# Image statistics on GpSimd, waiting rounds on ScalarE, and four circuit operations a step, in a diagonal LSTM with a quantum layer

## The chip, the cores and the metric

The kernel runs on one core of a Trainium2 chip. The metric is device time in microseconds, the median of the runs. Engines are named as in the profile: PE is TensorE's matrix products, PEld its weight loads, DVE is VectorE, ACT is ScalarE, POOL is GpSimd, SP is the engine that issues most of the DMAs. "L202" is line 202 of the kernel.

## The reference

The input x has the shape (16 images, 128 channels, 64 rows, 64 columns), all in float32. Two layers follow each other, each with a group norm in front and a residual around it.

```python
x = x + lstm(_gn(x), w_is, b_is, w_ss, b_ss)
x = x + quantum(_gn(x), pre_w, pre_b, q_weights, post_w, post_b)

def _gn(v, G=32, eps=1e-5):          # mean and variance over 4 channels and all pixels of an image
    ...
    return ((g - m) / jnp.sqrt(s + eps)).reshape(v.shape)

# layer 0: row i is shifted right by i columns (127 in all), then a scan over the columns
def step(carry, ist):
    h, c = carry
    h_shift = jnp.pad(h, ((0, 0), (0, 0), (1, 0)))[:, :, :-1]     # h of the row above
    s_s = einsum(w_ss[:, :, 0], h_shift) + einsum(w_ss[:, :, 1], h) + b_ss
    gates = ist + s_s                                             # ist = w_is @ column + b_is
    o, f, ig = sigmoid(gates[:, :3 * C]) in three parts
    g = jnp.tanh(gates[:, 3 * C:])
    c_new = f * c + ig * g
    h_new = o * jnp.tanh(c_new)

# layer 1: at each pixel four angles pre_w @ x + pre_b enter a circuit of four qubits with two
# layers of rotations (q_weights) and CNOTs; four expectation values go through post_w, post_b
```

Two facts matter here. First, row i sees i columns of zeros before its image begins. In these its state doesn't depend on the image: it is the same for all images and for all rows that still wait, and it follows from the biases and from the sum of the two taps of `w_ss`. Second, the rotations and the first CNOTs depend on `q_weights` alone, so a small matrix of amplitudes can be prepared once, at any time before layer 1 begins.

## The kernel before

**Preparation** (L220 to L430) loads the images into `ring`, a buffer of 40 rows an image; the 24 rows behind go through seven small buffers (three `rest` tiles and four `spare` tiles). On each 512-element piece VectorE runs `bn_stats` (L287), eight for an image; then `aggregated` (L290), one `bn_aggr` an image, turns the eight results into the mean and variance of a channel in `mv1`. SP's loads of the small buffers wait for the statistics that free them.

In the same stretch runs the chain of **waiting rounds**, `inv_step` (L191 to L212): round j takes the waiting rows' state j to state j+1. A state is one column of 128 channels in `hinv` and `cinv`. A round is eight products on TensorE (L199; two for each of four gates, since a float32 product takes two passes), four gate activations on ScalarE (L202, in the order f, i, g, o, the bias being a column operand), three one-column operations on POOL (L205 f·c, L206 i·g, L207 their sum), tanh of c (L209) and h = o·tanh(c) (L210, an Identity whose scale is the column of o). Behind each round's products stand two holding products, `keep` (L182), that keep TensorE busy; one reads a piece of the image in the ring, the other the weights `wsT`. 33 rounds (`EARLY`) are made here, spread over the images by a loop; later states are made inside the scan.

The order on every engine is the order in which the code issues (a manual schedule). So in the first round POOL first runs `coefficients` (L313 to L319) and the clearing of the state buffers (L366, L367), and only then the round's L205. ScalarE copies the transposed weights wxT, w0T and w1T (L326) behind the first round's h; TensorE transposes them into two alternating PSUM tiles, so that the third waits for the copy of the first.

At the **hand-over** POOL copies states 0 and 33 into the scan's h (L402, L403), TensorE makes the first step's products with them (L408), then three holding products (L182), then the group mean (L147), VectorE and ScalarE make 1/sqrt of the variance, and POOL normalises the first columns (L576, L588).

**The scan** has 160 steps in the skewed order. In a step TensorE makes the gate products (L783, L597), ScalarE copies and activates (L833, L802, L862), VectorE adds and multiplies (L798, L850, L858, L861, L868), POOL adds the residual (L641) and normalises the columns two steps ahead (L576 to L588). From step 33 on VectorE also takes three operations a step of the circuit (L441, L452, L470, L483), a generator of 120 operations: 8 rotations of 11, 4 CNOTs of 6, 8 products at the end. They stand behind the step's differences (L625) and in front of L798, which is the first of the chain that the step waits for. When four rows are finished, their statistics for the second norm (L732, 16 of them) are issued in the same place, up to six a step.

**Layer 1** then runs over all pixels, and stores.

Of the kernel before, what the change touches and what calls it, by code (L numbers as in the profile page):

```python
# [11 lines left out]
F32 = mybir.dt.float32  # L12
AF = mybir.ActivationFunctionType
# [3 lines left out]
P = 128  # L17
NB = 16
NH = 64
NW = 64  # L20
SLOTS = 32
# [4 lines left out]
BLOCK = ROWS * NW  # L26
CHUNK = 2 * BLOCK
EARLY = 33
FIRST = 8
STRIP = 4  # L30
FEW = 96
# [10 lines left out]
GO, GF, GI, GG = 0, 1, 2, 3  # L42
FUNC = {GO: AF.Sigmoid, GF: AF.Sigmoid, GI: AF.Sigmoid, GG: AF.Tanh}
# [38 lines left out]
def kernel(  # L82
# [16 lines left out]
    nc = tc.nc  # L99
# [10 lines left out]
    ring = const.tile([P, NB, RING * NW], F32, name="ring")  # L110
# [18 lines left out]
    w_image = const.tile([P, NB, 48], F32, name="w_image")  # L129
    b_image = const.tile([P, NB], F32, name="b_image")  # L130
    b_theta = const.tile([P, 1], F32, name="b_theta")
    w_amp = const.tile([P, 2, 128], F32, name="w_amp")
# [27 lines left out]
    small = ctx.enter_context(tc.tile_pool(name="small", bufs=2))  # L160
    with ExitStack() as scan:
# [4 lines left out]
        wsT = wpool.tile([P, 512], F32, name="wsT")  # L166
# [12 lines left out]
        def keep(pool, tag, v):  # L179

            ps = pool.tile([P, v.shape[-1]], F32, name=nc.get_next_instruction_name(), tag=tag)
            nc.tensor.matmul(ps, lhsT=wsT[:, 0:P], rhs=v, start=True, stop=True)  # L182
# [8 lines left out]
        def inv_step(j, pool):  # L191


            ps = {}
            rhs = hinv[:, j : j + 1].to_broadcast([P, P])
            for g in ORDER:
                ps[g] = pool.tile([P, P], F32, name=f"inv_ps{j}_{g}", tag=f"inv{g}")
                w = wsT[:, g * 128 : (g + 1) * 128]
                nc.tensor.matmul(ps[g], lhsT=w, rhs=rhs, start=True, stop=True)  # L199
            ac = small.tile([P, 4], F32, name=f"inv_a{j}", tag="inv_a")  # L200
            for g in ORDER:
                nc.scalar.activation(ac[:, g : g + 1], ps[g][:, 0:1], FUNC[g], bias=bias[:, g : g + 1])  # L202
            ig = small.tile([P, 2], F32, name=f"inv_i{j}", tag="inv_i")
            c = cinv[:, j + 1 : j + 2]
            nc.gpsimd.tensor_mul(ig[:, 0:1], ac[:, GF : GF + 1], cinv[:, j : j + 1])  # L205
            nc.gpsimd.tensor_mul(ig[:, 1:2], ac[:, GI : GI + 1], ac[:, GG : GG + 1])  # L206
            nc.gpsimd.tensor_add(c, ig[:, 0:1], ig[:, 1:2])  # L207
            th = small.tile([P, 1], F32, name=f"inv_t{j}", tag="inv_t")
            nc.scalar.activation(th, c, AF.Tanh)  # L209
            nc.scalar.activation(  # L210
                hinv[:, j + 1 : j + 2], th, AF.Identity, scale=ac[:, GO : GO + 1]
            )  # L212

        def above(v, a, b):

# [4 lines left out]
        with ExitStack() as prep:  # L220
# [68 lines left out]
            def aggregated(b):  # L289
                nc.vector.bn_aggr(  # L290
                    mv1[:, b, :], stats[:, b, 0:8].rearrange("p g s -> p (g s)")
                )


            q3 = qw.rearrange("p (n a) -> p a n", a=3)
            ang = pp.tile([P, 2, 3, 8], F32, name="ang")
            rnd = pp.tile([P, 2, 3, 8], F32, name="rnd")
# [14 lines left out]
            def coefficients():  # L312
                nc.gpsimd.tensor_mul(co[:, 0], trig[:, 0, 0, :], trig[:, 0, 2, :])  # L313
                nc.gpsimd.tensor_mul(co[:, 1], trig[:, 1, 0, :], trig[:, 0, 2, :])
                nc.gpsimd.tensor_mul(co[:, 2], trig[:, 0, 1, :], trig[:, 1, 2, :])
                nc.gpsimd.tensor_mul(co[:, 3], trig[:, 1, 1, :], trig[:, 1, 2, :])
                nc.gpsimd.tensor_scalar_mul(co[:, 4:8], co[:, 0:4], -1.0)
                nc.gpsimd.tensor_copy(cur[:, 0], expand)
                nc.gpsimd.memset(cur[:, 1], 0.0)  # L319

# [38 lines left out]
            for i in range(2):  # L359
                v = ws_n[i]  # L360
                nc.vector.tensor_add(sum_n[:, 2 * i : 2 * i + 2], v[:, :, 0::2], v[:, :, 1::2])
            transposed("wsT", wsT, lambda g: sum_n[:, g, :])
            biases()
            coefficients()
            for v in (*hst, *xns, none):
                nc.gpsimd.memset(v, 0.0)  # L366
            nc.gpsimd.memset(w_image, 0.0)  # L367

            for k in (3, 4, 0):
                statistics(0, k)  # L370
# [1 line left out]

            between = [angle_weights, output_weights]
            done = 0
            for b in range(NB):
                while b < NB - 1 and done * (NB - 1) < EARLY * (b + 1):
                    inv_step(done, ps_inv)
                    keep(ps_keep, "keep", ring[:, b, CHUNK : CHUNK + P])
                    keep(ps_keep, "keep", wsT[:, 0:P])
                    if done == 0:  # L380

                        transposed("wxT", wxT, lambda g: wx_n[:, g, :])
                        transposed("w0T", w0T, lambda g: ws_n[g // 2][:, g % 2, 0::2])
                        transposed("w1T", w1T, lambda g: ws_n[g // 2][:, g % 2, 1::2])
                    elif done > 4 and between:
                        between.pop(0)()
                    done += 1
                if b + 2 < NB:
                    rows(b + 2)
                if b + 1 < NB:  # L390
                    behind(b + 1)
                    for k in ORDERED:
                        statistics(b + 1, k)
                for k in (5, 6, 7):
                    statistics(b, k)
                aggregated(b)
            prep_ps.close()


# [373 lines left out]
        def step(t, ps):  # L773
# [36 lines left out]
            elif t:  # L810
                differences(t, now, diff)
                for g in summed:
                    half(g, 0, wsT, now[:, 0])
            if t > SLOTS:
                for _ in range(3):
                    next(steps, None)
            if t + 1 < SLOTS:

# [80 lines left out]
        with tc.manual_schedule():  # L899
            normalised(0)  # L900
            normalised(1)
            ps = gate_ps(0)
            for t in range(NSTEP):
                ps = step(t, ps)
            statistics(10.0, NSTEP)
            for later in sums:
                for _ in later:
                    pass
            residual(NSTEP - 1, hst[NSTEP % 2], nc.vector)
            low_rows(nc.sync, 6, spare[6])  # L910

            warm = small.tile([P, 1], F32, name="warm", tag="inv_t")
            nc.scalar.activation(warm, shift, AF.Sqrt)
            ps = ps_small.tile([P, 2, NB], F32, name="gm3", tag="small")

            def add(to, w, v, start=False):
                nc.tensor.matmul(to, lhsT=w, rhs=v, start=start, stop=True, skip_group_check=True)

            add(ps, by_half, moments, True)
            fill(2)  # L920
            for h in range(2):
                add(ps, by_half, added[:, :, :, h])
                add(ps[:, 1], by_one, inner[:, :, h])
            fill(1)

            v = block(NH - ROWS).rearrange("p i (r w) -> p i r w", w=NW)[:, :, :, NW - STRIP :]
            d, sq = (work.tile([P, NB, ROWS, STRIP], F32, name=f"strip{i}", tag=f"both{i}") for i in range(2))
            m = mean2.unsqueeze(2).unsqueeze(3).to_broadcast([P, NB, ROWS, STRIP])
            nc.vector.tensor_sub(d, v, m)
            nc.vector.tensor_mul(sq, d, d)  # L930
            for i, u in enumerate((d, sq)):
                u = u.rearrange("p i r w -> p i (r w)")
                nc.vector.reduce_sum(strip_sums[:, i], u, axis=mybir.AxisListType.X)
            add(ps, by_one, strip_sums)
# [24 lines left out]
            nc.tensor.matmul(ps, lhsT=w_theta, rhs=mr, start=True, stop=True)  # L959
            nc.vector.tensor_sub(b_image, b_theta.to_broadcast([P, NB]), ps)  # L960
# [219 lines left out]
```

## Time and profile before

| | us |
|---|---|
| median of 3 runs (1411.8 to 1412.43) | 1411.82 |
| the profiled execution | 1411.93 |
| its span, first to last instruction | 1409.8 |
| end of the last image's mean and variance (L290) | 94.54 |
| end of the state 33 (last L210 of the preparation) | 95.36 |
| first group mean (L147) | 100.48 |
| first step's normalised columns on TensorE (L597) | 103.98 |
| first circuit operation in the scan (L441) | 290.14 |
| last circuit operation (L483), start | 628.7 |

A line of the timeline gives the start in us from the beginning of the span, the duration in us, the engine, the line of the code, the operation, output and inputs by name, shapes, and how many neighbours are merged in the line; in brackets stand the idle time of the engine just before and what ended it. Since neighbours are merged, "x4" with 0.93 us is the time from the first one's start to the last one's end. In the first part of the page a row gives busy time, share of the span and number of instructions of each engine; in the fourth, shares of the chain of work that ended last.

A step of the scan in its wide middle takes 8.61 us (from one L625 to the next).

### The profile page before, as it was taken

The page shows a single profiled execution, that of the slowest core. Times are in us where ns is not written, and L with a number is a line of the kernel's source. Part 1 is how long each engine was busy: PE and PEld are TensorE (multiplying, and loading weights), DVE is VectorE, ACT ScalarE, POOL GpSimd, SP SyncE. Part 2 cuts the span into 40 slices and gives each one's busy share as a digit, 9 for nine tenths or more (in the row PEclk, how much of TensorE's full clock was granted, in tenths as well). Part 3 has the DMA queues.
Part 4 walks back from the last instruction along what each step waited for, and adds up shares of the span by engine and source line. Part 5 has one row for each costly group of instructions (what it writes and reads, how often), then busy time and mean ns, then how long its engine had stood idle before and what let it go on. Part 6 is the DMA issues. An engine that isn't in the chain of part 4 may idle for free.

```text
span 1409.8 us, 20064 instructions
## 1 busy us (share of the span) xinstructions
PE 1355.0 (96%) x6046; PEld 967.6 (69%) x6046; DVE 975.5 (69%) x2541; ACT 776.0 (55%) x1852; POOL 887.6 (63%) x1599
## 2 busy tenths in 40 slices
PE   6778999999999999999999999999999999999995
PEld 5658977777777766666677767777776787886332
DVE  7973565566665666887777776666665567876996
ACT  4655666555555555555555555555555566654331
POOL 4225777777777766777777776777777677763300
PEclk9999999999999999999999999999999999999998
DMA  9960000000000000133333100000000000014999
GB/s 339 407 234 2 1 1 1 1 0 1 0 1 1 1 1 1 60 120 120 120 120 120 60 1 1 1 1 0 1 1 0 1 0 1 1 31 143 383 400 358
DMA packets 64075, 107.04 MB, mean 76 GB/s; under 512 B 5040, under 2 KB 32720, under 8 KB 63968
## 3 DMA queue, kind: packets, MB, share of 16 engines
q1 hardware_dynamic: 59328, 94.39, 18.5%
q0 software_dynamic: 3408, 10.58, 2.0%
q8 instruction: 48, 0.79, 0.2%
q10 hardware_dynamic: 1232, 0.80, 0.2%
q14 instruction: 59, 0.48, 0.1%
HBM read 59.61 MB, written 46.14 MB: 75 GB/s over the span
## 4 chain that ended last, share of the span: by engine, by line
PE 82%; DVE 4%; ACT 1%; issue 1%; POOL 1%; DVEq 0%; ACTq 0%; POOLq 0%
PE ps L783 46%; PE ps L597 28%; PE po_None L1062 3%; PE theta_None L1011 2%; PE am_None L1040 1%; DVE spare L868 1%; DVE ps L858 1%; DVE ps L798 0%; DVE cst L861 0%; DVE stats L732 0%; ACT g L862 0%; ACT g L802 0%; PE po L1062 0%; DVE cst L850 0%; DVE ring L1080 0%
## 5 line engine op out<-in xcount | busy, mean ns | idle before, releaser
L597 PE MATMUL ps<-spare,wxT 128*128 128x512 f32 (+18 forms) x1280 | 479.7, 518 | 0.6 <-POOL spare L588 0.6
L798 DVE TENSOR_TENSOR ps<-ps,both 128x256 f32<-128x256 f32 (+9 forms) x536 | 219.1, 410 | 301.1 <-PE ps L783 299.5
L802 ACT ACTIVATE ps<-ps,bias 128x512 f32<-128x512 f32 (+23 forms) x480 | 279.1, 583 | 221.1 <-DVE ps L798 184.8
L783 PE MATMUL ps<-spare,w1T 128*128 128x256 f32 (+16 forms) x1272 | 346.8, 354 | 9.6 <-DVE spare L759 5.0
L597 PEld LDWEIGHTS ps<-spare,wxT 128*128 128x128 f32 x1280 | 231.1, 190 | 173.0 <-issue 155.4
L783 PE MATMUL ps<-spare,w0T 128*128 128x256 f32 (+16 forms) x1272 | 344.0, 352 | 0.0
L833 ACT COPY both<-ps 128x256 f32<-128x256 f32 (+9 forms) x536 | 189.6, 356 | 181.3 <-PE ps L783 161.7
L783 PEld LDWEIGHTS ps<-spare,w1T 128*128 128x128 f32 x1272 | 230.6, 190 | 36.5 <-DVE spare L868 7.2
L783 PEld LDWEIGHTS ps<-spare,wsT 128*128 128x128 f32 x1088 | 196.1, 190 | 80.4 <-DVE spare L868 30.1
L783 PE MATMUL ps<-spare,wsT 128*128 128x256 f32 (+14 forms) x1088 | 243.9, 366 | 2.6 <-DVE spare L868 1.2
L783 PEld LDWEIGHTS ps<-spare,w0T 128*128 128x128 f32 x1272 | 230.5, 190 | 21.0
L641 POOL TENSOR_TENSOR ring<-ring,spare 128x256 f32<-128x256 f32 (+15 forms) x375 | 231.5, 644 | 17.9 <-DVE spare L868 17.9
L588 POOL TENSOR_TENSOR spare<-spare,rstd 128x512 f32<-128x512 f32 (+10 forms) x160 | 170.9, 1068 | 14.8 <-DVE rstd L158 2.3
L582 POOL TENSOR_TENSOR spare<-ring 128x256 f32<-128x256 f32 (+13 forms) x165 | 139.8, 847 | 0.0
L862 ACT ACTIVATE g<-cst 128x256 f32<-128x256 f32 (+20 forms) x320 | 102.9, 368 | 65.5 <-DVE cst L861 65.1
L868 DVE TENSOR_TENSOR spare<-g,ps 128x256 f32<-128x256 f32 (+17 forms) x319 | 105.3, 368 | 44.8 <-ACT g L862 40.2
L576 POOL TENSOR_TENSOR spare<-ring,mean 128x256 f32<-128x256 f32 (+15 forms) x191 | 122.9, 644 | 5.6 <-DVE mean L148 5.4
L631 POOL TENSOR_TENSOR spare<-spare 128x240 f32<-128x240 f32 (+9 forms) x136 | 102.7, 755 | 36.4 <-DVE spare L868 32.8
L888 POOL COPY spare<-spare 128x16 f32<-128x16 f32 x64 | 21.0, 329 | 150.9 <-DVE spare L868 150.9
L802 ACT ACTIVATE g<-ps,bias 128x512 f32<-128x512 f32 (+20 forms) x160 | 97.3, 608 | 26.6 <-DVE ps L798 20.5
L861 DVE TENSOR_TENSOR cst<-cst,ps 128x256 f32<-128x256 f32 (+20 forms) x320 | 104.6, 368 | 5.5
L858 DVE TENSOR_TENSOR ps<-ps,g 128x512 f32<-128x512 f32 (+20 forms) x160 | 95.0, 594 | 18.8 <-ACT g L802 18.2
(370 smaller groups left out, 1096.4 us busy)
## 6 DMA issues: line engine op xcount, KB each, us to landing
out_dram<-ring SPq DMA_DIRECT2D x93, 256.0 KB, 4.8
ring<-in_x_dram SPq DMA_DIRECT2D x32, 512.0 KB, 7.6
low<-ring SPq DMA_DIRECT2D x6, 2048.0 KB, 7.5
ring<-in_x_dram SPq DMA_DIRECT2D x6, 2048.0 KB, 8.1
spare<-in_x_dram SPq DMA_DIRECT2D x27, 256.0 KB, 6.3
rest<-in_x_dram SPq DMA_DIRECT2D x21, 256.0 KB, 6.4
ring<-low POOLq DMA_DIRECT2D x18, 256.0 KB, 6.7
ring<-in_x_dram SPq DMA_DIRECT2D x16, 256.0 KB, 7.1
```

The costliest lines, as they stand in the source:

```text
L576: op = nc.gpsimd.tensor_sub(by_pairs(xn, 0, j0, j1), x0, over(mean1, j1 - j0))
L582: op = nc.gpsimd.tensor_sub(by_pairs(xn, 1, j0, j1), lower, of)
L588: nc.gpsimd.tensor_mul(v, v, r)
L597: nc.tensor.matmul(ps[g][:, :, a:b], lhsT=wxT[:, g * 128 : (g + 1) * 128], rhs=xns[t % 2][:, :, a:b], start=t > 0, stop=True, skip_group_c ...
L641: op = engine.tensor_add(x1, x1, by_pairs(new, q, j0, j1))
L783: nc.tensor.matmul(out, lhsT=w[:, g * 128 : (g + 1) * 128], rhs=rhs, start=False, stop=True, skip_group_check=True,)
L798: nc.vector.tensor_add(v, v, both[g][:, a:b])
L802: nc.scalar.activation(to[:, :, a:w], ps[g][:, :, a:w], FUNC[g], bias=bias[:, g : g + 1])
L833: nc.scalar.copy(both[g][:, a:b], ps[g][:, 0, a:b])
L858: nc.vector.tensor_mul(ig, ig, act[GG][:, :, a:w])
L861: nc.vector.tensor_add(c[:, q], c[:, q], ig[:, q])
L868: nc.vector.tensor_mul(new[:, q, a:v], th[:, q, a:v], act[GO][:, q, a:v])
```

## The change

There are four edits.

1. **The first norm's statistics.** `bn_aggr` stays on VectorE for images 0, 13, 14 and 15. Images 1 to 12 are taken on POOL by `gathering`, four images (`GATHER`) at a time, on views of the 16 means and 16 inner sums that `bn_stats` leaves for an image (each result has two halves of 256 elements): a tree of additions for the mean, deviations and their squares, plus the inner sums over 256, and a second tree. It is a generator of ten pieces of one or two operations; scratch is `w_amp`, which isn't used yet.
2. **Work behind POOL's share of a round.** `coefficients` and the clearing of buffers become generators as well. After each round `some` takes two pieces (in the first eight rounds) or three of whatever is first in the list `behind_pool`. The three lots of `gathering` enter the list after images 5, 9 and 13, which is after rounds 13, 21 and 30, counted from 0. What is left after the loop is issued then, ahead of the hand-over.
3. **The rounds.** f·c stays on POOL and is issued right after the f gate. i·g + f·c becomes one ScalarE instruction, an Identity with the scale column i and the bias column f·c, issued after all four gates. Both holding products of a round read `wsT`.
4. **The circuit.** Four operations a step in place of three, again from step 33 on.

```diff
+GATHER = 4
...
             for g in ORDER:
-                nc.scalar.activation(ac[:, g : g + 1], ps[g][:, 0:1], FUNC[g], bias=bias[:, g : g + 1])
-            ig = small.tile([P, 2], F32, name=f"inv_i{j}", tag="inv_i")
-            c = cinv[:, j + 1 : j + 2]
-            nc.gpsimd.tensor_mul(ig[:, 0:1], ac[:, GF : GF + 1], cinv[:, j : j + 1])
-            nc.gpsimd.tensor_mul(ig[:, 1:2], ac[:, GI : GI + 1], ac[:, GG : GG + 1])
-            nc.gpsimd.tensor_add(c, ig[:, 0:1], ig[:, 1:2])
-            th = small.tile([P, 1], F32, name=f"inv_t{j}", tag="inv_t")
-            nc.scalar.activation(th, c, AF.Tanh)
...
+                activate(ac[:, g : g + 1], ps[g][:, 0:1], FUNC[g], bias=bias[:, g : g + 1])
+                if g == GF:
+                    nc.gpsimd.tensor_mul(kept, ac[:, GF : GF + 1], cinv[:, j : j + 1])
+            activate(c, ac[:, GG : GG + 1], AF.Identity, scale=ac[:, GI : GI + 1], bias=kept)
+            activate(th, c, AF.Tanh)
+            activate(hinv[:, j + 1 : j + 2], th, AF.Identity, scale=ac[:, GO : GO + 1])
...
+            entries = stats[:, :, 0:8].rearrange("p b g (h s) -> p b (g h) s", s=3)
+            gathered, within = (
+                w_amp[:, 0, k * P // 2 : (k + 1) * P // 2].rearrange("p (i e) -> p i e", i=GATHER)
+                for k in range(2)
+            )
+
+            def gathering(b0):
+                b1 = b0 + GATHER
+                means, inners = entries[:, b0:b1, :, 1], entries[:, b0:b1, :, 2]
+                m, var = (mv1[:, b0:b1, k] for k in range(2))
+
+                def total(to, v):
+                    n = 8
+                    while n > 1:
+                        nc.gpsimd.tensor_add(gathered[:, :, 0:n], v[:, :, 0:n], v[:, :, n : 2 * n])
+                        v, n = gathered, n // 2
+                        yield
+                    nc.gpsimd.tensor_add(to.unsqueeze(2), v[:, :, 0:1], v[:, :, 1:2])
+                    nc.gpsimd.tensor_scalar_mul(to, to, 1.0 / 16)
+                    yield
+
+                yield from total(m, means)
+                nc.gpsimd.tensor_sub(gathered, means, m.unsqueeze(2).to_broadcast([P, GATHER, 16]))
+                nc.gpsimd.tensor_mul(gathered, gathered, gathered)
+                yield
+                nc.gpsimd.tensor_scalar_mul(within, inners, 1.0 / BLOCK)
+                nc.gpsimd.tensor_add(gathered, gathered, within)
+                yield
+                yield from total(var, gathered)
...
-            coefficients()
-            for v in (*hst, *xns, none):
-                nc.gpsimd.memset(v, 0.0)
-            nc.gpsimd.memset(w_image, 0.0)
+
+            def cleared():
+                for v in (*hst, *xns, none, w_image):
+                    nc.gpsimd.memset(v, 0.0)
+                    yield
...
+            behind_pool = [coefficients(), cleared()]
+
+            def some():
+                for later in behind_pool[:1]:
+                    if [next(later, True) for _ in range(2 if done < 8 else 3)][-1] is not None:
+                        behind_pool.pop(0)
...
                     inv_step(done, ps_inv)
-                    keep(ps_keep, "keep", ring[:, b, CHUNK : CHUNK + P])
+                    some()
+                    keep(ps_keep, "keep", wsT[:, 0:P])
                     keep(ps_keep, "keep", wsT[:, 0:P])
...
-                aggregated(b)
+                if b in (0, *range(13, NB)):
+                    aggregated(b)
+                if b in (5, 9, 13):
+                    behind_pool.append(gathering(b - GATHER))
+            for later in behind_pool:
+                for _ in later:
+                    pass
             prep_ps.close()
...
-            if t > SLOTS:
-                for _ in range(3):
+            if SLOTS < t:
+                for _ in range(4):
                     next(steps, None)
```

`coefficients` gets two `yield`s, which cut it into three pieces; its operations stay the same.

More of the change, by code (lines that the diff above doesn't have):

```diff
@@ L200, in inv_step, with activate @@
             ac = small.tile([P, 4], F32, name=f"inv_a{j}", tag="inv_a")
-            for g in ORDER:
-                nc.scalar.activation(ac[:, g : g + 1], ps[g][:, 0:1], FUNC[g], bias=bias[:, g : g + 1])
-            ig = small.tile([P, 2], F32, name=f"inv_i{j}", tag="inv_i")
-            c = cinv[:, j + 1 : j + 2]
-            nc.gpsimd.tensor_mul(ig[:, 0:1], ac[:, GF : GF + 1], cinv[:, j : j + 1])
-            nc.gpsimd.tensor_mul(ig[:, 1:2], ac[:, GI : GI + 1], ac[:, GG : GG + 1])
-            nc.gpsimd.tensor_add(c, ig[:, 0:1], ig[:, 1:2])
-            th = small.tile([P, 1], F32, name=f"inv_t{j}", tag="inv_t")
[L209 to L212, printed above, removed]
+            kept = small.tile([P, 1], F32, name=f"inv_k{j}", tag="inv_k")
+            c = cinv[:, j + 1 : j + 2]
+            th = small.tile([P, 1], F32, name=f"inv_t{j}", tag="inv_t")
+            def activate(to, v, func, **of):
+                nc.scalar.activation(to, v, func, **of)
+            for g in ORDER:
+                activate(ac[:, g : g + 1], ps[g][:, 0:1], FUNC[g], bias=bias[:, g : g + 1])
[4 more added lines that the diff above has]
+            activate(hinv[:, j + 1 : j + 2], th, AF.Identity, scale=ac[:, GO : GO + 1])
         def above(v, a, b):
@@ L317, in coefficients @@
                 nc.gpsimd.tensor_scalar_mul(co[:, 4:8], co[:, 0:4], -1.0)
+                yield
                 nc.gpsimd.tensor_copy(cur[:, 0], expand)
@@ L363 @@
             biases()
-            coefficients()
-            for v in (*hst, *xns, none):
-                nc.gpsimd.memset(v, 0.0)
-            nc.gpsimd.memset(w_image, 0.0)
+            def cleared():
+                for v in (*hst, *xns, none, w_image):
+                    nc.gpsimd.memset(v, 0.0)
+                    yield
             for k in (3, 4, 0):
```

## The prediction

> **What bounds the kernel now.** I read the page first (busy shares, then the chain that ended last), next the table of windows over the first 100 us, then the timeline of one waiting round, of the hand-over to the scan and of the first round, and last VectorE's timeline of the scan where the circuit's steps meet the second statistics.
>
> ```profile
> PE 1355.0 (96%) x6046; PEld 967.6 (69%) x6046; DVE 975.5 (69%) x2541; ACT 776.0 (55%) x1852; POOL 887.6 (63%) x1599
> PE 82%; DVE 4%; ACT 1%; issue 1%; POOL 1%; DVEq 0%; ACTq 0%; POOLq 0%
> ```
>
> TensorE sets the scan, so a change of small operations can pay only where TensorE waits: before the scan begins, and in scan steps that VectorE makes late. The diff touches both.
>
> In the first 95 us the window table shows two candidates. VectorE is busy 9.93 of 10 us from 40 on (statistics), the DMA engines are full (1.04, 402 to 408 GB/s) from 30 to 90; and the waiting rounds run as one chain:
>
> ```profile
> 83.46 1.16 PE L199 MATMUL inv_ps<-hinv,wsT 128*128 128x128 f32 x8 [0.46 <-ACT hinv L210]
> 83.99 0.93 ACT L202 ACTIVATE inv_a<-inv_ps,bias 128x1 f32<-128x1 f32 x4 [0.58 <-PE inv_ps L199]
> 84.39 0.19 POOL L205 TENSOR_TENSOR inv_i<-inv_a,cinv 128x1 f32<-128x1 f32 x1 [1.54 <-ACT inv_a L202]
> 84.77 0.19 POOL L206 TENSOR_TENSOR inv_i<-inv_a 128x1 f32<-128x1 f32 x1 [0.19 <-ACT inv_a L202]
> 85.05 0.19 POOL L207 TENSOR_TENSOR cinv<-inv_i 128x1 f32<-128x1 f32 x1
> 85.27 0.20 ACT L209 ACTIVATE inv_t<-cinv 128x1 f32<-128x1 f32 x1 [0.35 <-POOL cinv L207]
> 85.51 0.29 ACT L210 ACTIVATE hinv<-inv_t,inv_a 128x1 f32<-128x1 f32 x1
> ```
>
> One round is products, four gates, three POOL operations, tanh, h: the next products start at 85.85, so 2.39 us a round, and 31 of the 33 rounds have that rhythm (two longer because of other work). Which candidate ends last?
>
> ```profile
> 94.17 0.37 DVE L290 BATCH_NORM_AGGREGATE mv<-stats 128x2 f32<-128x48 f32 x1
> 95.07 0.29 ACT L210 ACTIVATE hinv<-inv_t,inv_a 128x1 f32<-128x1 f32 x1
> 95.42 0.19 POOL L402 COPY spare<-hinv 128x1 f32<-128x1 f32 x1 [0.49 <-ACT hinv L210]
> 95.78 0.49 PE L408 MATMUL ps<-spare,w1T 128*128 128x128 f32 x2 [0.83 <-POOL spare L403]
> 97.67 0.81 PE L182 MATMUL I-1369_1370<-rest,wsT 128*128 128x384 f32 x2
> 100.48 0.40 PE L147 MATMUL gm<-mv,wide_sb 128*128 128x16 f32 x2
> ```
>
> The last image's mean and variance are there at 94.54, but the group mean (L147) that reads them stands on TensorE behind the first step's products (L408) and three holding products (L182), and those wait for the last h at 95.36 and its copies on POOL. So the statistics have 5.9 us to spare; the rounds and POOL's copies set the start of the scan. Everything later follows them.
>
> **What the Trainium skill says.** (1) "ScalarE: Activation LUTs", section "What ACT_TABLE_LOAD costs": a [128,1] operand for scale or bias adds about 93 ns each, and neighbours overlap by about 93 ns. The trace agrees for one operand: tanh without takes 0.202 us, h with a scale 0.295; the gates of the first round, ready together, follow at 0.15 us with a duration of 0.26. Both operands in one instruction are in no row. (2) "SBUF — State Buffer", "Who interferes with whom": a VectorE operation with two inputs in SBUF waits for a POOL operation that reads SBUF. Agreed: the circuit's L452 takes 0.22 us alone and 0.7 to 0.89 beside POOL, while statistics, with one input, keep 0.34 in the scan. (3) "TensorE: Matmul & The Clock Gate", Part 1: half rate until one window of about 3.4 us has been busy. The trace has single products at 0.421 us up to 20.2 and about 0.275 after, 3.3 us after the idle gap that ends at 16.87.
>
> **The change, part by part.**
>
> *The first round.*
>
> ```profile
> 14.46 0.74 POOL L367 MEMSET w_image<- 128x768 f32 x1
> 15.17 0.19 POOL L205 TENSOR_TENSOR inv_i<-inv_a,cinv 128x1 f32<-128x1 f32 x1
> 16.25 0.57 ACT L326 COPY wxT<-wxT_ps 128x512 f32<-128x512 f32 x1
> 16.87 1.13 PE L325 MATMUL w1T_ps<-ident,spare 128*128 128x128 f32 x4 [0.62 <-ACT wxT L326]
> ```
>
> Today POOL is in coefficients and clearing until 15.20, although the first gate is done at 13.62. The copy of wxT stands on ScalarE behind that round's h (16.34), and w1T's transposes wait for the copy. With clearing spread over rounds 2 to 5, h ends at about 14.9, the copy starts when wxT's transposes end (15.39), so 15.45, and w1T's transposes follow TensorE's own queue at 16.07: 0.8 us earlier. Round 1 at half rate gives 0.16 back (its gates come at 0.427 us, so the old POOL chain was done 0.15 after the last gate, the new c, tanh order needs 0.31). But the idle gap in front of 16.87 is gone, so full rate can come a window earlier, and round 1 then takes 2.35 instead of 2.94. From 0.6 to 1.4 us; I take 1.0.
>
> *The rounds.* Two POOL operations go; c = g·i + f·c becomes one ScalarE instruction behind the fourth gate. f·c is ready at 84.58, no wait. The fourth gate starts at 84.66 (83.99 plus three times (0.93 - 0.26)/3). c starts 0.15 later, at 84.81, and takes 0.202 + 2 x 0.093 = 0.39: 85.20; tanh 0.033 later (the gap from L209's end to L210's start), 85.23 instead of 85.27. That is 0.04 us a round, 1.2 us over 30 rounds. Bounds: if the second operand is read beside the first, c takes 0.295 and a round gains 0.13 (4.0 in all); if c starts only when the o gate has ended, a round loses 0.11 (3.2). I take 0.04, which the rows price term by term.
>
> *POOL's aggregation.* 14 operations for four images, three times. VectorE loses twelve times 0.29 us (its start-to-start cost), which buys nothing: it would wait for the full DMA engines, and it was not last. What counts is POOL's queue. Rounds 14 to 17 and 22 to 25 hold ten pieces each; at up to 2.1 us a round they end 0.1 us before the next f·c. The third lot enters after round 30: three pieces in round 31, three in round 32, and the last four after it, all ahead of L402. Their prices, start to start with the wait for the result before, are those of the second norm's sums on POOL (L711 to L714): 0.33 for 32 elements, 0.40 for 64, 0.45 for a scaling of 64; and 0.27 for one column (L206 to L207). Round 32's pieces: 0.28 + 0.27 + 0.40 + 0.28 + 0.45 + 0.40 = 2.1. The tail: 0.33 + 0.30 + 0.28 + 0.28 + 0.27 = 1.5. They begin 1.08 us after the round's products do and end at 4.6, so the copy that needs h goes at 4.7 instead of 2.40 (95.42 - 93.02): 2.3 us lost, the same wait in a new place. From 1.8 to 2.7. The statistics are still not last.
>
> Sum for the start of the scan: 1.0 + 1.2 - 2.3 = -0.1, so 0.1 us later.
>
> *The holding product* reads wsT instead of the image: same size, no row shows it waiting after round 1; nothing.
>
> *The circuit.* 120 VectorE operations from step 33 on, three a step, so through step 72; by four they end at step 62.
>
> ```profile
> 591.93 2.10 DVE L452 SCALAR_TENSOR_TENSOR amp<-amp,co,amp 128x8 f32<-128x8 f32 x3
> 593.96 2.04 DVE L732 BATCH_NORM_STATS2 stats<-ring 128x6 f32<-128x256 f32 x6
> 595.92 1.07 DVE L798 TENSOR_TENSOR ps<-ps,both 128x256 f32<-128x256 f32 x3
> 636.54 2.05 DVE L732 BATCH_NORM_STATS2 stats<-ring 128x6 f32<-128x256 f32 x6
> 639.18 0.43 DVE L798 TENSOR_TENSOR ps<-ps,both 128x256 f32<-128x256 f32 x1 [0.59 <-PE ps L783]
> ```
>
> In steps 68 to 72 circuit and statistics together outlast the products: L798 starts without idle time. Without the circuit it waits 0.59 for TensorE. Those five steps take 44.66 us (L625 at 591.53 to 636.19); five at the usual 8.615 take 43.07: 1.6 us gained. The fourth operation in steps 33 to 62 lies in the idle time before L798, 1.74 us in most steps, 0.92 where two operations met POOL; it costs 0.22 to 0.89. Hidden, just: nothing, at worst 0.3 in eight steps.
>
> Sum: 1411.9 (the profiled execution: span 1409.8 and 2.1 around it) + 0.1 - 1.6 = 1410.4; the median shown is 0.1 lower, so 1410.3.
>
> **Rivals.** *A, the forecast:* rounds almost as long as before, POOL's tail eats the early start, the circuit pays. With the bounds of its terms 1408.6 to 1412.0. *B, the rounds really shorten:* c costs one operand's price, 0.13 a round. For it: copies at L339 follow each other at 0.063 us, so much of an instruction overlaps; against it: gates with a bias follow at 0.15, so an operand isn't free. 1.2 (first round) + 4.0 - 2.3 + 1.6 = 4.5: 1407.3. *C, slower:* ScalarE holds c back until the o gate has finished, which the old order didn't need since POOL worked beside it. Place: between L202's last and tanh; price 0.11 x 30 = 3.2, so 1411.8 - 1.6 - 0.8 + 3.2 + 2.3 = 1414.9. It decides once c starts more than 0.1 us after the 84.81 of my sum. Against it: L202's rows overlap, and c reads g and i, not o. *D, the fourth circuit operation delays L798:* 0.3 us in eight or more steps takes the gain of 1.6 back: 1412.5.
>
> **How the numbers follow.** A 0.63, B 0.26, C 0.06, D 0.05. The time is A's, 1410.3; the range runs from B, 1407.3, to A's late end and D, 1412.4, and leaves out C and half of what lies below B. A measurement of this kernel tells 0.2%, 2.8 us: faster means below 1409.0. B nearly whole and a tenth of A: 0.31. Slower is C: 0.05. Between them 0.64.
>
> **What would show it.** Round to round from 2.39 to 2.35; c at about 0.39 us; the copy of h 2.3 us after h with POOL busy until then; the first group mean near 100.6; steps 68 to 72 at 8.6; gaps before L798 above zero in steps 33 to 62. Wrong if c takes 0.3 us or starts after o's end, if POOL's last pieces are done before h, or if steps 33 to 62 grow beyond 8.62.

## The result and the profile after

The changed kernel takes 1410.74 us in the median of 14 runs (1408.24 to 1412.8), the kernel before 1411.84 in 14 runs (1410.46 to 1412.62). The ratio is 0.9992 with a 95% interval of 0.9984 to 1.0: about 1 us faster, within what counts as the same. The forecast was 1410.3. The profiled run of the changed kernel took 1412.27 with a span of 1410.5, near the slow end of its runs, and it shows why they spread.

In what follows L200 and L207 are the rounds' products and ScalarE's operations (one helper line for all of them), L212 is f·c, L453 and L454 are the copies of h, L459 the first step's products, L148 the group mean, L503 and L492 the circuit, L783 the second statistics, L849 the first addition of a step's chain.

The first part of the page and the chain:

```profile
PE 1355.5 (96%) x6046; PEld 967.5 (69%) x6046; DVE 978.5 (69%) x2529; ACT 786.2 (56%) x1885; POOL 885.7 (63%) x1575
...
PE 84%; DVE 3%; ACT 1%; issue 1%; POOL 1%; DVEq 0%; ACTq 0%; POOLq 0%
```

TensorE is as busy as before and still sets the end; VectorE is a little less often the one that came last (3% of the chain, 4% before). Changes of this size are seen only stage by stage. First a round, from the timeline of the changed kernel:

```profile
85.76 1.16 PE L200 MATMUL inv_ps<-hinv,wsT 128*128 128x128 f32 x8 [0.42 <-ACT hinv L207]
86.29 0.93 ACT L207 ACTIVATE inv_a<-inv_ps,bias 128x1 f32<-128x1 f32 x4 [0.58 <-PE inv_ps L200]
86.69 0.19 POOL L212 TENSOR_TENSOR inv_k<-inv_a,cinv 128x1 f32<-128x1 f32 x1 [2.15 <-ACT inv_a L207]
87.12 0.38 ACT L207 ACTIVATE cinv<-inv_a,inv_k 128x1 f32<-128x1 f32 x1
87.52 0.20 ACT L207 ACTIVATE inv_t<-cinv 128x1 f32<-128x1 f32 x1
87.76 0.29 ACT L207 ACTIVATE hinv<-inv_t,inv_a 128x1 f32<-128x1 f32 x1
```

c takes 0.38 us with its two column operands, and tanh starts 1.76 us after the round's products (87.52 - 85.76), where it started 1.81 after them before. The next products are at 88.11: 2.35 us a round in place of 2.39.

The first round, from the timeline of the changed kernel, and from that of the kernel before:

```profile
16.41 0.75 PE L361 MATMUL w1T_ps<-ident,spare 128*128 128x128 f32 x4
16.99 1.06 PE L200 MATMUL inv_ps<-hinv,wsT 128*128 128x128 f32 x8
19.34 1.16 PE L200 MATMUL inv_ps<-hinv,wsT 128*128 128x128 f32 x8 [0.52 <-ACT hinv L207]
...
17.79 1.91 PE L199 MATMUL inv_ps<-hinv,wsT 128*128 128x128 f32 x8
20.73 1.16 PE L199 MATMUL inv_ps<-hinv,wsT 128*128 128x128 f32 x8
```

TensorE no longer waits for the copy of wxT, and the second round's eight products (round 1, counted from 0) take 1.06 us in place of 1.91, since the clock is already at full rate. Round 2 begins at 19.34, 7.78 us after the first round's products (11.56); it was 9.52 (20.73 - 11.21).

The hand-over, from the timeline of the changed kernel:

```profile
92.44 0.29 ACT L207 ACTIVATE hinv<-inv_t,inv_a 128x1 f32<-128x1 f32 x1
...
93.20 0.32 POOL L324 TENSOR_TENSOR w_amp<-w_amp 128x64 f32<-128x64 f32 x1
93.60 0.83 POOL L312 TENSOR_TENSOR w_amp<-w_amp 128x32 f32<-128x32 f32 x3
94.51 0.20 POOL L315 TENSOR_TENSOR mv<-w_amp 128x4 f32<-128x4 f32 x1
94.80 0.22 POOL L316 TENSOR_SCALAR mv<-mv 128x4 f32<-128x4 f32 x1
...
95.08 0.32 POOL L453 COPY spare<-hinv 128x16 f32<-128x16 f32 x2
95.57 0.80 PE L459 MATMUL ps<-spare,w1T 128*128 128x128 f32 x2 [3.20 <-POOL spare L454]
...
99.15 1.49 PE L183 MATMUL I-1366_1367<-rest,wsT 128*128 128x384 f32 x2
103.13 0.40 PE L148 MATMUL gm<-mv,wide_sb 128*128 128x16 f32 x2
```

The last h ends at 92.74, but the copy that needs it starts at 95.21, behind the last pieces of POOL's third lot. TensorE idles 3.20 us for it. And then its products are slow: a holding product of 384 columns takes 1.49 us and took 0.81. The table of windows says why (its columns: window, length, busy time of PE, PEld, DVE, ACT and POOL, granted clock, DMA share, GB/s):

```profile
84.00:92.40 8.40, 6.90 (x46) 5.37 (x44) 8.37 (x15) 6.44 (x27) 2.11 (x10) 1.00 0.95 366
92.40:95.57 3.17, 0.00 (x0) 0.00 (x0) 2.81 (x6) 1.59 (x3) 2.54 (x11) 0.90 0.01 5
95.57:103.13 7.56, 7.38 (x23) 4.71 (x23) 0.00 (x0) 0.00 (x0) 0.00 (x0) 0.59 0.00 0
```

In the gap TensorE does nothing, and its clock falls: by the record of the granted clock in the same trace it is halved at 94.91, 2.53 us after the last product ended (92.38), and full again at 101.73. Over the chain that follows the gap 0.59 of full speed is granted. From the first product to the group mean 7.56 us pass (103.13 - 95.57), where it was 4.70 (100.48 - 95.78).

The scan, from VectorE's timeline of the changed kernel: a step with the fourth circuit operation in its worst place, and a step with statistics.

```profile
293.00 2.34 DVE L503 SCALAR_TENSOR_TENSOR amp<-amp_in,co,amp 128x16 f32<-128x16 f32 x3
295.47 0.43 DVE L849 TENSOR_TENSOR ps<-ps,both 128x256 f32<-128x256 f32 x1
...
594.47 2.04 DVE L783 BATCH_NORM_STATS2 stats<-ring 128x6 f32<-128x256 f32 x6
596.94 0.43 DVE L849 TENSOR_TENSOR ps<-ps,both 128x256 f32<-128x256 f32 x1 [0.42 <-PE ps L834]
```

At 295.35 the circuit is done, 0.12 us before L849 starts. It fits: L849 comes 3.07 us after the step's first L676, as L798 came 3.07 us after L625 before the change. At 596.94 VectorE waits for TensorE again, 0.42 us. The five steps from 68 on take 42.87 us (L676 at 594.07 to 636.94) in place of 44.66.

So the two profiled spans, 1409.85 and 1410.47, differ like this (each term from the two timelines):

| stretch | before | after | after less before |
|---|---|---|---|
| start of the span to the first round's products | 11.21 | 11.56 | +0.35 |
| to round 2's products | 9.52 | 7.78 | -1.74 |
| to the end of the last h | 74.63 | 73.40 | -1.23 |
| to the copy of that h | 0.06 | 2.47 | +2.41 |
| to the first step's product | 0.36 | 0.36 | 0.00 |
| to the first normalised columns' product | 8.20 | 11.27 | +3.07 |
| to the end | 1305.87 | 1303.64 | -2.23 |

The sum is +0.63. The first term is loads that land at other times in every run (11.1 to 11.7 in the runs below). The times of the two runs differ by less, 0.34, because the time that lies outside the span fell too, from 2.08 to 1.80 us. That isn't chance: in every run whose span was taken it is 2.0 to 2.2 us in the kernels that make c on POOL (the kernel before, before_circ4 and two_oldc below) and 1.7 to 1.9 in all others, but for two runs of hold (2.4 and 3.4). So making c on ScalarE gains another 0.3 us that no stretch of the timeline shows; where it arises is open.

### The profile page after: what moved, and what is told of

It is laid out like the page before. It is cut to its first block, busy times and chain, and to the rows that moved or that the text cites. A ratio compares the mean times of both kernels' runs of the same rounds, so it can differ in the third digit from the quotient of the medians.

```text
span 1410.5 us, 20068 instructions
## 1 busy us (share of the span) xinstructions
PE 1355.5 (96%) x6046; PEld 967.5 (69%) x6046; DVE 978.5 (69%) x2529; ACT 786.2 (56%) x1885; POOL 885.7 (63%) x1575
## 4 chain that ended last, share of the span: by engine, by line
PE 84%; DVE 3%; ACT 1%; issue 1%; POOL 1%; DVEq 0%; ACTq 0%; POOLq 0%
PE ps L834 47%; PE ps L648 29%; PE po_None L1112 3%; PE theta_None L1061 2%; PE am_None L1090 1%; DVE spare L919 0%; DVE ps L909 0%; PE po L1112 0%; DVE cst L912 0%; DVE ps L849 0%; DVE ring L1130 0%; ACT g L853 0%; ACT g L913 0%; DVE stats L783 0%; DVE cst L901 0%
## 5 line engine op out<-in xcount | busy, mean ns | idle before, releaser
L849 DVE TENSOR_TENSOR ps<-ps,both 128x256 f32<-128x256 f32 (+9 forms) x536 | 219.9, 411 | 295.4 <-PE ps L834 291.5
```

The source lines that it names most:

```text
L849: nc.vector.tensor_add(v, v, both[g][:, a:b])
```

## Experiments

Each kernel was timed beside the kernel before on its chip; ratios are to that. Where the place of the last h is compared, it is counted from the first round's products, to take out the first term of the table: 84.15 us before, 81.18 in the changed kernel. The last column is that time.

| kernel | median us | before, us | ratio (95%) | last h |
|---|---|---|---|---|
| the changed kernel | 1410.74 | 1411.84 | 0.9992 (0.9984 to 1.0) | 81.18 |
| hold: twelve holding products | 1412.86 | 1411.66 | 1.0009 (1.0002 to 1.0015) | 81.19 |
| hold5: five | 1409.24 | 1411.02 | 0.9987 (0.9979 to 0.9995) | 81.44 |
| two_lots | 1406.63 | 1411.66 | 0.9965 (0.9952 to 0.9977) | 80.98 |
| no_lots | 1406.23 | 1411.66 | 0.9965 (0.9952 to 0.9977) | 81.19 |
| lots_earlier | 1406.36 | 1411.06 | 0.9964 (0.9952 to 0.9977) | 81.05 |
| two_circ3 | 1409.10 | 1411.66 | 0.9982 (0.9974 to 0.9989) | 81.20 |
| before_circ4 | 1409.40 | 1411.06 | 0.9988 (0.9981 to 0.9994) | 83.28 |
| two_oldc | 1409.09 | 1411.02 | 0.9984 (0.9977 to 0.9992) | 82.61 |
| two_early | 1406.97 | 1411.02 | 0.9970 (0.9958 to 0.9981) | 82.96 |
| two_cfirst | 1406.03 | 1411.02 | 0.9962 (0.9950 to 0.9975) | 81.36 |
| two_nohold | 1403.62 | 1411.06 | 0.9945 (0.9932 to 0.9957) | 81.78 |
| no_nohold | 1403.34 | 1411.06 | 0.9945 (0.9931 to 0.9958) | 81.55 |

### POOL's pieces behind the last round

**two_lots** takes the third lot from POOL:

```diff
-                if b in (0, *range(13, NB)):
+                if b in (0, *range(9, NB)):
                     aggregated(b)
-                if b in (5, 9, 13):
+                if b in (5, 9):
```

> Images 9 to 12 go back to VectorE, so nothing of POOL's stands behind the last round. Theory (POOL's queue held the hand-over): the copy of h follows h by 0.06 us, 2.4 us are gained on a fast run of the changed kernel, and TensorE has no idle gap long enough for its clock to fall: median about 1406, spread under 2 us. Rival (statistics on VectorE are last or nearly so, four more on it push the group mean out): 1408 or more, and the group mean waits for VectorE's last aggregation.

1406.63: the theory's number. The copy of h starts at 92.49, 0.06 after h, and the group mean is at 97.54, behind the holding products; the last aggregation ended at 94.13.

**no_lots** takes all three lots away; `aggregated(b)` runs for every image.

> All sixteen images aggregated on VectorE, none on POOL. Theory (the aggregation on POOL buys nothing, since VectorE waits for the loads at the end anyway): the same as with two lots within 0.5 us, about 1406, last aggregation at the same place near 94.5. Rival (POOL's lots relieve a VectorE that is nearly full): eight more aggregations of 0.29 us on VectorE make the last one 1 to 2.3 us later, and the time 0 to 2 us longer than with two lots.

1406.23, the same, and the last aggregation ends at 94.06, with 16 of them on VectorE as with 8 (94.13). Aggregating on POOL gains nothing here.

**lots_earlier** leaves all of POOL's work where it is, but lets each lot begin one image earlier:

```diff
-                if b in (5, 9, 13):
-                    behind_pool.append(gathering(b - GATHER))
+                if b in (4, 8, 12):
+                    behind_pool.append(gathering(b - GATHER + 1))
```

> All three lots stay on POOL, but each enters the list one image earlier (after images 4, 8, 12), so the third has four rounds for its ten pieces and only its last piece, 0.55 us, stands behind the last f times c. Theory (the loss is only the pieces behind the last round, not the work on POOL): the copy of h follows h at once, and the time is that of two lots, 1406 to 1407. Rival (POOL's 42 operations cost in the rounds themselves, or beside VectorE's statistics): 1408 or more, with longer rounds where pieces stand.

1406.36, again the same. POOL's timeline of lots_earlier in the last round:

```profile
90.85 0.19 POOL L212 TENSOR_TENSOR inv_k<-inv_a,cinv 128x1 f32<-128x1 f32 x1 [1.38 <-ACT inv_a L207]
90.99 0.20 POOL L315 TENSOR_TENSOR mv<-w_amp 128x4 f32<-128x4 f32 x1
91.28 0.22 POOL L316 TENSOR_SCALAR mv<-mv 128x4 f32<-128x4 f32 x1
91.56 0.20 POOL L453 COPY spare<-hinv 128x16 f32<-128x16 f32 x1
92.33 0.19 POOL L453 COPY spare<-hinv 128x1 f32<-128x1 f32 x1 [0.58 <-ACT hinv L207]
```

One piece is left after the last f·c; POOL then idles 0.58 us for h. So the 42 operations cost nothing while rounds cover them, and what the changed kernel loses is the queue behind the last round. By the ratios (0.9992 and 0.9964) the two kernels are 4.0 us apart, more than the 2.4 us of the wait itself. For the rest I suspected the clock.

### The clock behind the gap

**hold** fills the gap with twelve holding products after the loop:

```diff
+            for _ in range(12):
+                keep(ps_keep, "keep", wsT[:, 0:P])
             prep_ps.close()
```

> Theory: after the last round TensorE idles about 3.2 us behind POOL's last pieces, and in some runs its clock then falls to half rate for the first step's products and the holding products, which costs up to 2.9 us; that is why the changed kernel's runs spread from 1408.2 to 1412.8. Twelve more holding products (2.7 us) in that gap keep the clock: all runs at the fast end, 1408 to 1409, copies of h still about 2.4 us after h, first products after them at 1.8 us for the eight and not 3.4. Rival (the spread comes from elsewhere, such as the memory or the scan): median stays near 1410.7 and the spread stays 4 us.

It missed: 1412.86. The clock stayed, the first step's products ran at full rate, but a holding product took 0.545 us from start to start and not the 0.224 that I had counted; each waits for the one before. All write the same PSUM tile, which may be the reason; no run changed the tile. They ended at 98.65, and the first step's product came at 98.80 in place of 95.57. **hold5** is the same with five.

> As the kernel with twelve holding products, but five: there one took 0.545 us, since all write one PSUM tile, and the twelve ran 3.2 us past the copies of h. Five take 2.7 us and end just before the copies, about 95.0. Theory (half rate after the idle gap is what spreads the changed kernel's runs): every run at the fast end, median 1408.3 to 1409.3, the group mean near 100.3 and not 103.1. Rival (the spread comes from elsewhere): median near 1410.7 as without them, with runs from 1408 to 1413.

TensorE's timeline of hold5:

```profile
94.67 0.49 PE L183 MATMUL I-1357_1358<-wsT 128*128 128x128 f32 x2
95.62 0.49 PE L461 MATMUL ps<-spare,w1T 128*128 128x128 f32 x2 [0.47 <-POOL spare L456]
...
97.51 0.81 PE L183 MATMUL I-1381_1382<-rest,wsT 128*128 128x384 f32 x2
...
100.32 0.40 PE L148 MATMUL gm<-mv,wide_sb 128*128 128x16 f32 x2
```

And the window behind the gap, with the columns as above:

```profile
95.60:103.10 7.50, 6.95 (x31) 4.02 (x32) 1.29 (x7) 0.63 (x2) 0.22 (x1) 1.00 0.00 0
```

The copies are as late as in the changed kernel (95.26), but the clock stays at 1.00, and the group mean follows the first product by 4.70 us, as before the change, and comes at 100.32. That the half rate costs 2.9 us in the profiled run is shown: in the eleven other profiles with the three holding products, none of which has a gap over 0.9 us there, the same stretch takes 4.67 to 4.70.

How often it happens can be read from the mean granted clock, which was taken with every run of the changed kernel. It is 0.995 or 0.996 in the five fastest runs (1408.24 to 1409.14 us) and 0.994 or 0.993 in the other nine (1410.41 to 1412.8). An estimate from the trace: half rate for 6.82 us of a span of 1410 lowers the mean by 0.0024. Among all other runs with a recorded clock (92 of the kernel before, 125 of the kernels below and above) only three lie below 0.995: hold5's slowest, from 1410.88 to 1411.41 us, at 0.994. So nine of 14 runs lost the clock, and they are the nine slowest: this is what spreads them. With five holding products three of 14 lost some of it; none of these was profiled, and why is open. So hold5's median is 1409.24, but its runs still reach from 1407.89 to 1411.41, and its interval overlaps that of the changed kernel. The narrow band that I expected came only in kernels without the gap (two_lots: 1405.68 to 1406.81).

### The circuit

**two_circ3** is two_lots with `range(3)` in the scan, **before_circ4** the kernel before with `range(4)`.

> Two lots, and the circuit back at three operations a step. Theory: steps 68 to 72 again take about 44.7 us in place of 42.9, so 1.6 to 1.8 us more than the kernel with two lots, about 1407.8. Rival (the fourth operation costs elsewhere what it saves there, or the steps would even out): no difference to two lots beyond 0.5 us.

> The kernel before with one edit, the circuit at four operations a step. Theory: steps 68 to 72 fall from 44.7 to about 42.9 us, nothing else moves, so 1.6 to 1.8 us below the kernel before, a ratio near 0.9988. Rival (the gain belongs to the other edits): ratio 1.0000 within 0.0003.

The edit pays from both sides, by about as much: before_circ4 is 0.12% below the kernel before (1.7 us), two_circ3 0.17% above two_lots (2.5 us, where the profiled spans behind the first normalised columns differ by 1.4: 1305.03 and 1303.59). VectorE's timeline of before_circ4 in a step that used to be late:

```profile
599.68 2.05 DVE L732 BATCH_NORM_STATS2 stats<-ring 128x6 f32<-128x256 f32 x6
602.33 0.43 DVE L798 TENSOR_TENSOR ps<-ps,both 128x256 f32<-128x256 f32 x1 [0.60 <-PE ps L783]
```

With the circuit gone, VectorE is done with the statistics 0.60 us before TensorE's product that L798 needs.

### The rounds

**two_oldc** makes c on POOL again, in two_lots:

```diff
-            activate(c, ac[:, GG : GG + 1], AF.Identity, scale=ac[:, GI : GI + 1], bias=kept)
+            ig = small.tile([P, 1], F32, name=f"inv_i{j}", tag="inv_i")
+            nc.gpsimd.tensor_mul(kept, ac[:, GF : GF + 1], cinv[:, j : j + 1])
+            nc.gpsimd.tensor_mul(ig, ac[:, GI : GI + 1], ac[:, GG : GG + 1])
+            nc.gpsimd.tensor_add(c, kept, ig)
```

> Two lots, with c made by three POOL operations again. Theory: a round takes 2.39 us and not 2.345, so the last h comes 1.3 to 1.5 us later, and the median is about 1408.0 against 1406.6 with two lots. Rival (the shorter round comes from the lighter POOL queue or the holding product on other data, not from c on ScalarE): rounds stay at 2.35 and the time at 1406.6.

Rounds take 2.39 us (two of them 2.56), and the last h comes 1.6 us later (82.61 against 80.98): c on ScalarE is what shortens them, though by 0.05 us each. The median moved by 2.7 us by the ratios, more than this; 0.3 of it lies outside the span (2.09 us in two_oldc, 1.80 in two_lots), and the rest isn't placed.

**two_cfirst** issues c as soon as g is there, ahead of the o gate:

```diff
+                if g == GG:
+                    activate(c, ac[:, GG : GG + 1], AF.Identity, scale=ac[:, GI : GI + 1], bias=kept)
-            activate(c, ac[:, GG : GG + 1], AF.Identity, scale=ac[:, GI : GI + 1], bias=kept)
```

> Two lots, with c issued on ScalarE ahead of the o gate, which is needed only for h. Theory (ScalarE's own queue sets the round: c waits for nothing but the g gate and f times c): c starts about 0.1 us earlier, a round falls from 2.345 to about 2.27, the last h comes 2.4 us earlier, near 90.0, and the median is about 1404.2; the last aggregation near 94.1 still ends before the group mean. Rival (c with two column operands blocks ScalarE so long that o ends when tanh would have started anyway): rounds at 2.34 and no gain.

The rival was right but for 0.01 us: rounds take 2.33 us. ScalarE's timeline of two_cfirst, in a round whose products start at 59.92:

```profile
60.44 0.71 ACT L207 ACTIVATE inv_a<-inv_ps,bias 128x1 f32<-128x1 f32 x3 [0.58 <-PE inv_ps L200]
61.24 0.39 ACT L207 ACTIVATE cinv<-inv_a,inv_k 128x1 f32<-128x1 f32 x1
61.54 0.24 ACT L207 ACTIVATE inv_a<-inv_ps,bias 128x1 f32<-128x1 f32 x1
61.68 0.19 ACT L207 ACTIVATE inv_t<-cinv 128x1 f32<-128x1 f32 x1
```

g ends at 61.15, c starts at 61.24, 1.33 us into the round and only 0.03 earlier than behind the o gate (87.12 - 85.76 is 1.36), since it waits for g. The o gate now stands between c and tanh, and tanh starts 1.76 us into the round, as in the changed kernel.

### The first round

**two_early** runs `coefficients` and `cleared` in one piece ahead of the first f·c, in two_lots.

> Two lots, with coefficients and clearing back in one piece ahead of the first round's f times c. Theory: h of round 0 comes 1.3 us later, the copy of wxT and w1T's transposes follow, TensorE idles in front of them again and reaches full rate near 20 instead of 16.4; round 2 begins 1.7 us later and the median is about 1408.2. Rival (only the wait for the copy counts, not the clock): 0.8 us later, about 1407.4, full rate still near 16.5.

TensorE's timeline of two_early:

```profile
16.89 1.13 PE L361 MATMUL w1T_ps<-ident,spare 128*128 128x128 f32 x4 [0.63 <-ACT wxT L362]
17.81 1.92 PE L200 MATMUL inv_ps<-hinv,wsT 128*128 128x128 f32 x8
...
20.91 1.16 PE L200 MATMUL inv_ps<-hinv,wsT 128*128 128x128 f32 x8 [0.21 <-ACT hinv L207]
```

The profile is the theory's: the old wait for the copy of wxT, round 1's products at half rate, full rate at 20.4, the last h 2.0 us later than in two_lots. The median isn't: 1406.97, 0.3 us above two_lots (0.7 by the ratios), which is within the noise. The profiled run is the slowest of its six (1407.94; the others go down to 1406.68). Full rate comes at different times in the same order: before_circ4 has the old first round too, with the same idle gap of TensorE (16.48 to 17.10), but by the clock's record full rate came at 16.63, inside that gap, and round 2 began 8.65 us after the first products and not 9.52 or 9.69. So the gap alone doesn't delay the clock. In the eleven profiles with the new first round the same stretch takes 7.57 to 8.35 us. So spreading the clearing is worth between 0.3 and 2 us, by where the clock happens to rise.

### What the group mean waits for

**two_nohold** is two_lots, **no_nohold** is no_lots, both without the three holding products ahead of the group mean:

```diff
-            for v in (rests[NB - 2][0], rests[NB - 2][2], rests[NB - 1][0]):
-                keep(ps_small, "small", v[:, 0 : 3 * P])
```

> Two lots, without the three holding products ahead of the group mean. In it TensorE was done with the first step's products near 94.6, the last aggregation ended at 94.1, and the group mean came at 97.5 behind the holding products. Theory (these products, not the statistics, hold the group mean): group mean near 94.7, 2.8 us earlier, median near 1403.7. Rival (they keep the clock, or the statistics are later than seen): TensorE at half rate in the chain of the norm or the group mean behind the aggregation, 1405.5 or more.

> No lots on POOL, without the three holding products. Here the last aggregation is the next that the group mean could wait for, so POOL's lots have their best chance. Theory (VectorE waits for the loads at the end, so eight more aggregations ahead of it change nothing): last aggregation at 94.0 to 94.6, time within 0.5 us of the kernel with two lots and no holding products. Rival (aggregation on VectorE is late by its own 2.3 us): 1 to 2.3 us more than that kernel.

1403.62 and 1403.34, the fastest kernels of this study, 0.55% below the kernel before. The hand-over in two_nohold:

```profile
93.34 0.37 DVE L293 BATCH_NORM_AGGREGATE mv<-stats 128x2 f32<-128x48 f32 x1
...
93.51 0.49 PE L459 MATMUL ps<-spare,w1T 128*128 128x128 f32 x2 [0.78 <-POOL spare L454]
...
95.40 0.29 PE L148 MATMUL gm<-mv,wide_sb 128*128 128x16 f32 x2
```

The group mean follows the first step's products without a wait, at full rate, 1.7 us after the last aggregation. Even here the sixteen aggregations on VectorE end in time (93.75 in no_nohold, 1.2 us before the group mean). Part of what POOL's lots save on VectorE only becomes longer waiting for loads: between 20 and 95 us it waits for them 2.6 us in two_nohold and 1.3 in no_nohold.

## Why the prediction was right, and where its sum was not

*What bounds.* That the statistics had room and the hand-over was set by the rounds and by POOL's copies is confirmed by no_lots: eight more aggregations on VectorE than in two_lots change nothing.

*The first round*, taken at 1.0 of 0.6 to 1.4: the profiled run gained 1.74, since the first products at full rate came at 16.6 in place of 20.4. two_early puts the gain lower, 0.3 to 0.7 in the medians. The reason given for the second part, that without the idle gap full rate comes a window earlier, doesn't hold: in before_circ4 it came inside the gap. The term was one of chance more than I said; 1.0 lies between.

*The rounds*, 1.2: the profile has 1.23, and c the 0.38 us of the sum with both operands priced in full. (Of the 32 intervals from round to round before the change 29 are of 2.39 us; three are longer and not two.) What the edit also took off outside the span, 0.3 us, the sum put at nothing by adding 2.1 us to both spans. Rival B (one operand free, 1407.3) and rival C (c after o's end, 1414.9) both fall: c starts 0.16 us after the fourth gate's start, before its end.

*POOL's tail*, 2.3 lost: 2.41 in the profile; the pieces behind the last round were priced from the second norm's sums. lots_earlier shows that the place was the cause.

*The circuit*, 1.6: 1.79 in the five steps, 1.7 by before_circ4. The fourth operation, hidden with 0.92 us at hand and up to 0.89 to place: 0.12 us were left in the tightest step shown, and steps 33 to 62 stayed at 8.61. Rival D falls.

*What the sum missed.* "A" had POOL's tail move the copy and nothing else. But TensorE has no work while the copy waits, and the Trainium skill names a window of about 3.4 us, free-running, after which an idle TensorE falls to half rate ("TensorE: Matmul & The Clock Gate", Part 1). I used that page for the first round alone. The trace agrees that the window runs freely: the clock's changes at 16.40, 94.91 and 101.73 us lie 23 and 2 times 3.41 us apart. It differs from the page in how much idleness is enough, and the measurement decides: the fall came 2.53 us after the last product, and the 3.41 us before it still held 0.8 us of products. Where the window's edge lies in the gap changes from run to run, which would explain why nine runs lost the clock and five did not; this is argued, as only one of them was profiled.

Half rate costs 2.86 us up to the group mean in the profiled run, which is why that run is 2.0 us above the forecast. Other terms erred the other way: the first round gained 0.7 us more in that run than forecast, the stretch behind the first normalised columns 0.6 more (2.23 for 1.6), the time outside the span 0.3. So the five runs that kept the clock lie 1.2 to 2.1 us below the forecast and the other nine above it. The copies' queue, the rounds and the circuit were sized rightly, but that the median met the number to 0.4 us is luck: a cost that the sum left out and gains that it undercounted nearly cancel.

*Its own sums.* Two figures don't follow from its terms, and no reading here rests on them: with 1.4 us for the first round and 1.8 for POOL's tail A's early end is 1409.4, not 1408.6, and D's 0.3 us in eight steps takes 2.4 us and not 1.6, which gives 1412.7, not 1412.5.

*What stays open:* why three of hold5's runs show a lower clock although the gap is filled; what makes the 0.3 us outside the span; and the part of two_oldc's and two_circ3's medians above their profiles. The 0.4 us of the 2.23 that were gained outside steps 68 to 72 are no more than this stretch varies: it takes 1302.62 to 1304.02 us in the twelve profiles with four operations a step.

## What to carry to other kernels

Work that is put on an idle engine costs nothing as long as its last piece ends before that engine is next needed on the path: look at what is queued behind the last piece, and let the lots begin earlier rather than make them smaller. Price a new wait twice, once for the engine that waits and once for the clock of a TensorE that has nothing to do meanwhile. Before an engine that is busy all the time is relieved, see what it waits for at the end: VectorE was full here, and sixteen aggregations or eight made no difference, while three holding products in front of the mean held 2.8 us.

## What the runs showed that was not expected

- By the clock's record full rate of TensorE came between 15.05 and 17.76 us in the eleven profiles with the new first round, at 16.63, 20.13 and 20.22 in the three with the old one: the same order of instructions doesn't fix it.
- After one gap of 3.2 us the clock was halved for 6.82 us, two windows of 3.41, although TensorE was at work again 0.66 us after the fall.
- A holding product of 128 columns into the PSUM tile that the one before has just written takes 0.545 us from start to start, while the rounds' products into four tiles follow each other at 0.224 for the same two passes.
- Moving an instruction ahead in ScalarE's queue gained 0.01 us a round: it could start only 0.03 us earlier, 0.09 us after the gate it reads had ended, and the gate that it overtook then delayed its reader by as much.
